# Attention's memory by last use, the second image's tokens in six tiles, the sum check among the experts, and three key pairs at first

## The chip, the cores and the metric

The kernel runs on one core of a Trainium2 chip. A core has five engines with a queue of instructions each: TensorE (PE, matrix products and transposes, with its own queue part PEld for loading the stationary operand), VectorE (DVE), ScalarE (ACT), GpSimd (POOL) and SyncE (SP, which here only issues DMA transfers). Engines wait for one another through semaphores. SBUF is the on-chip memory of 128 partitions, PSUM the banks that PE writes its products to, DRAM the memory outside. The metric is the device time of one execution in microseconds (us). The kernel before took 2222.04 us, the median of 4 runs between 2219.52 and 2223.07.

## What is computed

The input is two images of 256 channels and 56 x 56 pixels. Three blocks follow each other, each added to its input:

```python
x = x + conv_attention(group_norm(x))          # 1x1 conv to q,k,v; 3x3 depthwise conv; 7x7 neighbourhood
                                               # attention, 4 heads with dilation 1, 4 with 2; projection
t = to_tokens(x)                               # (2, 3136, 256)
t = t + linear_attention(layer_norm(t))
t = t + experts(layer_norm(t))                 # 8 experts, the best 2 of each token, H = 1024
x = from_tokens(t)

# linear_attention(x), per image, with h = 8 heads of 32:
Q = elu(x @ Wq) + 1;  K = elu(x @ Wk) + 1;  V = x @ Wv
KV = einsum('nshd,nshv->nhdv', K, V)           # one 32x32 matrix per head and image, over all tokens
Z = 1 / (einsum('nlhd,nhd->nlh', Q, K.sum(1)) + 1e-6)
msg = layer_norm(einsum('nlhd,nhdv,nlh->nlhv', Q, KV, Z) @ Wm)
msg = layer_norm(relu(concat(x, msg) @ W1) @ W2)
return x + msg
```

What matters below is that the linear attention of an image can take up its queries only when the keys of all that image's tokens are summed.

## The kernel before

The kernel has four stages. The *front* (`front()`, to about 810 us) does group norm, convolutions and neighbourhood attention in bands of rows, strip by strip. A finished strip is divided by its sums (`normalise`, whose reciprocals are stored to DRAM as `rb` at L567), projected on PE into a PSUM tile `s_ps` together with the input `x_s` (loaded at L758, transposed at L323), copied to `t_i` by DVE or ACT in turn (`evac`, L154) and stored as tokens to the DRAM array `td` (L772). There are 49 blocks of 128 tokens. The first 25 (`NA`) are the first image's, with half a block of the second. While the front finishes the second image, the first image's tokens are loaded again (`t_a`) and their keys are made (`first_keys`, L295).

The *keys* of two blocks, a pair, are made by `keys()` (L228), a generator in three parts: statistics on DVE, `rs` as a power on POOL (L225), the normalised `xt`, its transposes `pts` on PE and the copy to `xT_b`; then the product `kp` with `w_k` and `elu`+1 of it, `ks`; then the products `kx` of `ks` and `xt`, which PE sums up over the pairs in one PSUM tile, and the sum of `ks` in `acc` on POOL. `close_keys` and `merged` (L284, L1175) turn the sums into the two small matrices that queries use: transposes `kxt`, products with `w_v` (`kvt`, masked by DVE into `kvt_sb`), products with `w_m` (`mwp`), centred, and the diagonal blocks `ksm`. PE and DVE alternate there.

Between the front and the next stage stands `check_sums` (L821): it loads all stored reciprocals as `chk_r` (128 x 396), compares them with two bounds in four DVE operations, sums over the partitions with one product `chk_p` and writes a flag `bad`, read at the very end.

*Layer 1* (`layer1`, L1081, from 810 to about 1380 us) loads the second image's tokens into one tile `t_b` of 24 blocks by six transfers on SP (L199), its weights by transfers on POOL's queue (L1104), prepares the feed-forward's weights (`centre(fw2)`, the bias products `hb`, the scaling of `fw1`, L1140 to L1152), merges the first image's sums and then works on 14 groups of up to four blocks in a software pipeline of 18 steps (L1443). In step s, group s is in its queries (`q`: products `pq`, `elu`, then `pd` and the quotient), group s-1 in the message (`m`: products `pm` in L1262, then transposes `mts`), s-2 in the feed-forward (`f`), s-3 in routing (`r`), whose last part, the rows' scattering, comes in the step after (`p`). In each of the first six steps two key pairs of the second image (`u` and `v`) are made as well, and at the end of step 5 the second image's sums are closed and merged. PE's instructions stay in the order in which the program calls the parts (`manual_schedule`, L1441); this order is a string, one letter for each next part:

```python
for part in "mqfpufmuqfurfvrfvfv" if s < ng else "mfffpmfrfrff":
    next(on.get(part, iter(())), None)
```

A letter with no generator in this step does nothing. The first `pm` product of a step marks where it starts. The other engines' instructions are put in order by a scheduler of the framework.

The *experts* (loop at L1648, 53 tiles of 256 rows from about 1381 to 2146 us) gather rows (`xr`), transpose them (`px`), scale them (`xe`, DVE), multiply by `w1e` (`ph`, L1626) and `w2e` (`py`, L1634), add the bias (`yt`, DVE) and scatter the result. The last stage transposes the output back.

SBUF and PSUM are shared out in pools. A pool that closes frees its memory, and a later pool may lie on it. Where a later pool has nothing said of it, its first use waits for everything that ever used the memory beneath the whole pool; with `reuse_waits="tile"` a tile waits only for what used its own bytes. The front's pools (L342 to L350) and its two PSUM pools close together at its end; `rtb` and `p3w`, `p3k`, `p3s`, with the PSUM pools `p3pk`, `p3pa`, `p3pq`, `p3ph`, lie on their memory. The pools of the experts' weights have `reuse_waits="tile"` already.

## Time and profile before

| | us |
|---|---|
| median of 4 runs (2219.52 to 2223.07) | 2222.04 |
| the profiled execution | 2219.14 |
| its span, first to last instruction | 2217.4 |
| PE busy in the span (90%) | 2002.8 |
| DVE / ACT / POOL busy | 1016.2 / 620.2 / 688.7 |
| mean granted clock of PE | 0.952 |

By stage, from one answer on the engines' busy time in stretches (PE busy of the stretch's length, granted clock, share of the DMA engines):

| stretch, us | length | PE busy | clock | DMA |
|---|---|---|---|---|
| 0 to 776, front | 776.0 | 686.7 | 0.95 | 0.39 |
| 776 to 810, end of the front | 34.0 | 28.2 | 0.95 | 0.17 |
| 810 to 1381, layer 1 | 571.0 | 497.9 | 0.93 | 0.15 |
| 1381 to 2146, experts | 765.0 | 753.8 | 1.00 | 0.65 |
| 2146 to 2217.4, output | 71.4 | 36.3 | 0.61 | 0.61 |

How to read the profile: each line of a timeline gives the start of an instruction (or of several alike), its length, engine, line of the program, operation and operands by the program's names, and in brackets how long the engine had been idle before it and what released it. `SPq` and `POOL ... DMA_DIRECT2D` are issues of transfers; the time when the data land is another. A busy time of PE includes stretches at a lower granted clock, in which the same product takes up to twice as long; the clock column tells of these.

### The profile page before, as it was taken

Reading aid. Unit: us, or ns where it says so; the run is one execution under the profiler, and the core shown is the slowest. Engines: PE = TensorE matmul, PEld = TensorE weight load, DVE = VectorE, ACT = ScalarE, POOL = GpSimd, SP = SyncE. Lnnn points to the kernel's source line nnn. Section 1 sums busy time; section 2 is a strip of 40 time slices with the busy share of each in tenths; the row PEclk is TensorE's granted clock in tenths of the full one; section 3 lists DMA queues with packets and bytes.
Section 4 is the critical chain, followed back from the end, with each engine's and each line's share of the span. In section 5 each row is a group of like instructions: output and inputs, shape, how many; then the busy total and the mean of one; then the engine's idle time right before and its main releaser. Section 6 shows DMA issues by size and latency. Waiting matters only on the chain. (4 is left out here: it accounts for less than half of the span.)

```text
span 2217.4 us, 27966 instructions
## 1 busy us (share of the span) xinstructions
PE 2002.8 (90%) x10188; PEld 1403.7 (63%) x10188; DVE 1016.2 (46%) x2506; ACT 620.2 (28%) x1240; POOL 688.7 (31%) x806
## 2 busy tenths in 40 slices
PE   4899889999988867999999984999999999999994
PEld 2454444554444545666565673888888888888873
DVE  4877867875976544455455443211111111111111
ACT  1233323333323312433323321222222222222221
POOL 3821102111023423445344453223223333233320
PEclk9999989999989988999999996999999999999995
DMA  7642422343341140000011113866666666666627
GB/s 164 146 106 82 128 71 68 107 127 83 108 148 28 44 141 3 10 29 34 34 49 50 46 57 121 273 186 192 185 189 200 183 197 188 183 199 189 190 58 238
DMA packets 187682, 267.92 MB, mean 121 GB/s; under 512 B 24502, under 2 KB 146180, under 8 KB 187166
## 3 DMA queue, kind: packets, MB, share of 16 engines
q1 hardware_dynamic: 157374, 220.64, 32.1%
q0 software_dynamic: 21568, 31.26, 7.1%
q10 hardware_dynamic: 8592, 14.11, 2.4%
q8 instruction: 84, 1.38, 0.3%
q14 instruction: 64, 0.52, 0.1%
HBM read 199.02 MB, written 73.34 MB: 123 GB/s over the span
## 5 line engine op out<-in xcount | busy, mean ns | idle before, releaser
L1626 PE MATMUL ph<-xe,w1e 128*128 128x256 f32 x1696 | 379.7, 382 | 11.2 <-DVE xe L1618 11.2
L1634 PE MATMUL py<-w2e,hT 128*128 128x256 f32 x1696 | 374.7, 379 | 0.0
L1626 PEld LDWEIGHTS ph<-xe,w1e 128*128 128x128 f32 x1696 | 321.4, 191 | 60.8 <-DVE xe L1618 17.8
L1634 PEld LDWEIGHTS py<-w2e,hT 128*128 128x128 f32 x1696 | 322.2, 190 | 43.8
L1630 ACT ACTIVATE hT<-ph,sv 128x256 f32<-128x256 f32 x360 | 168.1, 473 | 488.1 <-PE ph L1626 485.7
L508 DVE SCALAR_TENSOR_TENSOR yc<-ypad,w,yc 128x1120 f32<-128x1120 f32 x192 | 267.8, 1398 | 50.9 <-ACT yc L506 47.9
L495 PE MATMUL pc<-ypad,diag 128*128 128x448 f32 x432 | 176.6, 549 | 0.5 <-ACT ypad L489 0.5
L1639 DVE TENSOR_TENSOR yt<-py,b2e 128x512 f32<-128x512 f32 x53 | 36.7, 692 | 303.8 <-PE py L1634 303.8
L145 POOL DMA_INDIRECT y<-yt,idi x106 | 167.2, 1577 | 26.1 <-issue 17.2
L483 PE MATMUL py<-x_sb,wq 128*128 128x448 f32 (+1 forms) x384 | 158.9, 545 | 17.5 <-ACT ypad L489 9.8
L539 DVE TENSOR_TENSOR p<-s_ps,tab 98x340 f32<-98x340 f32 (+5 forms) x240 | 138.1, 601 | 62.1 <-PE s_ps L535 60.3
L1641 POOL TENSOR_SCALAR yt<-yt,eq 128x256 f32<-128x256 f32 x106 | 49.4, 472 | 372.0 <-DVE yt L1639 372.0
L544 ACT ACTIVATE p<-p 98x680 f32<-98x680 f32 (+5 forms) x120 | 111.8, 932 | 170.2 <-DVE p L539 163.5
L535 PE MATMUL s_ps<-qT,kT 32*98 32x170 f32 (+5 forms) x960 | 129.8, 405 | 19.2 <-DVE p L539 17.3
L1600 DVE CAST idi<-xr 128x2 int32<-128x2 f32 x53 | 9.0, 169 | 289.9 <-DMA y<-yt,idi 289.9
L535 PEld LDWEIGHTS s_ps<-qT,kT 32*98 32x98 f32 (+1 forms) x960 | 57.2, 171 | 106.8 <-DVE p L539 60.8
L483 PEld LDWEIGHTS py<-x_sb,wq 128*128 128x128 f32 x384 | 71.5, 200 | 82.5 <-issue 55.5
L495 PEld LDWEIGHTS pc<-ypad,diag 128*128 128x128 f32 x432 | 78.2, 189 | 71.6 <-issue 68.2
L472 POOL TENSOR_SCALAR diag<-ident,w 128x128 f32<-128x128 f32 x108 | 84.0, 796 | 117.4 <-PE pc L495 110.4
L145 POOL DMA_INDIRECT xs<-row,si x98 | 96.3, 983 | 64.7 <-DVE si L1418 36.0
L225 POOL TENSOR_TENSOR rs<-rs,mhalf 128x2 f32<-128x2 f32 (+2 forms) x89 | 65.2, 739 | 117.4 <-DVE rs L224 107.2
L1292 PE MATMUL p<-m2T,fw 128*128 128x512 f32 (+2 forms) x224 | 95.2, 549 | 0.0
(281 smaller groups left out, 2635.8 us busy)
## 6 DMA issues: line engine op xcount, KB each, us to landing
w1e<-in_L_ffn_W SPq DMA_DIRECT2D x53, 1024.0 KB
w2e<-in_L_ffn_W SPq DMA_DIRECT2D x53, 1024.0 KB
yd<-yc SPq DMA_DIRECT2D x24, 784.0 KB
xr<-xs SPq DMA_DIRECT2D x53, 260.0 KB
ld<-yd SPq DMA_DIRECT2D x28, 448.0 KB
b2e<-in_L_ffn_b SPq DMA_DIRECT2D x53, 128.0 KB
yr<-y SPq DMA_DIRECT2D x12, 512.0 KB
out<-o_sb ACTq DMA_DIRECT2D x24, 256.0 KB
```

Source lines behind the costliest of these rows:

```text
L145: ins = nc.gpsimd.indirect_dma_start(out=dst[:, :], out_offset=bass.IndirectOffsetOnAxis(ap=index, axis=0), in_=src, in_offset=None, **kw,)
L472: nc.gpsimd.tensor_scalar(diag[:, tap, :], ident, w2[:, oc, tap : tap + 1], 1.0, ALU.mult, ALU.mult)
L483: nc.tensor.matmul(py[:, :n, :], wq1[:, ct, oc * P : (oc + 1) * P], x_sb[:, ct, (q0 + g0) * WW : (q0 + g0 + n) * WW], start=(ct == 0), sto ...
L495: nc.tensor.matmul(pc, diag[:, tap, :], ypad[:, dy : dy + 8, dx : dx + WW], start=(tap == 0), stop=(tap == 8),)
L508: nc.vector.scalar_tensor_tensor(yc[:, 8:, :], src, w, yc[:, 8:, :], ALU.mult, ALU.add)
L535: nc.tensor.matmul(s_ps[:nk, j, :n].rearrange("p (i j) -> p i j", j=nj), kT[hs], q[hs], start=True, stop=True,)
L539: nc.vector.tensor_tensor(p[:nk, 2 * pr : 2 * pr + 2, :n].rearrange("p h (i j) -> p h i j", j=nj), s_ps[:nk, :, :n].rearrange("p h (i j) - ...
L544: nc.scalar.activation(p[:nk, :, :n], p[:nk, :, :n], AF.Exp)
L1292: nc.tensor.matmul(p1[:, :w], fw1[:, k, oc * P : (oc + 1) * P], rhs, start=(k == 0), stop=(k == 3))
L1626: nc.tensor.matmul(p1, w1e[:, ct, j * P : (j + 1) * P], xe[:, ct, :], start=(ct == 0), stop=(ct == 1),)
L1630: nc.scalar.activation(hT[:, j, :], p1, AF.Gelu, bias=sv[:, 4 + j : 5 + j])
L1634: nc.tensor.matmul(py[:, h, :], hT[:, j, h * P : (h + 1) * P], w2e[:, j, :], start=(j == 0), stop=(j == NJ - 1),)
```

## The change

The diff does five things.

- The front's pools are declared in another order: `p2b` and `p2r` behind the pools of loaded rows, keys, values and tables. `rtb` and all pools of layer 1 get `reuse_waits="tile"`, and the four PSUM pools are declared in another order.
- `t_b` becomes a list of six tiles of four blocks; `at()` picks the tile.
- `check_sums` is called in the loop over expert tiles, ahead of tile 4, takes its tiles from the experts' pools (its product in the tag `pt`), and `bad` lies in the pool of constants.
- What prepared the feed-forward's weights becomes `prepare_feed_forward()`, called behind the parts of step 0.
- The second image's 12 key pairs come three in each of the steps 0 and 1, with the strings "quvuqvuvwww" and "mquvumvquwvww", and two in each of the steps 2, 3 and 4; the sums are closed and merged at the end of step 4 instead of 5.

```diff
--- before.py
+++ after.py
@@ -187,8 +187,10 @@
 
         def at(self, n0, n):
 
-            h = int(n0 >= NA)
-            return self.t[h][:, n0 - h * NA : n0 - h * NA + n, :]
+            if n0 < NA:
+                return self.t[0][:, n0 : n0 + n, :]
+            k = (n0 - NA) % 4
+            return self.t[1][(n0 - NA) // 4][:, k : k + n, :]
 
         def turned(self, n0, n):
 
@@ -339,14 +341,15 @@
 
 
         cv = ExitStack()
-        bp = ph.enter_context(tc.tile_pool(name="p2b", bufs=1))
+
         tbp = ph.enter_context(tc.tile_pool(name="p2t", bufs=1))
         ldp = ph.enter_context(tc.tile_pool(name="p2l", bufs=2))
         kp = ph.enter_context(tc.tile_pool(name="p2k", bufs=3))
         vp = ph.enter_context(tc.tile_pool(name="p2v", bufs=2))
         pp = ph.enter_context(tc.tile_pool(name="p2p", bufs=2))
+        rp_ = ph.enter_context(tc.tile_pool(name="p2r", bufs=1))
+        bp = ph.enter_context(tc.tile_pool(name="p2b", bufs=1))
         ac = ph.enter_context(tc.tile_pool(name="p2ac", bufs=2))
-        rp_ = ph.enter_context(tc.tile_pool(name="p2r", bufs=1))
         xp = ph.enter_context(tc.tile_pool(name="p2x", bufs=2))
         cw = cv.enter_context(tc.tile_pool(name="p1w", bufs=1, side="right"))
         yp = cv.enter_context(tc.tile_pool(name="p1y", bufs=2, side="right"))
@@ -818,28 +821,24 @@
         tokens.kw.close()
         return tokens
 
-    def check_sums():
-
-        cp = ctx.enter_context(tc.tile_pool(name="chk", bufs=1))
-        with ExitStack() as ph:
-            wp = ph.enter_context(tc.tile_pool(name="chk2", bufs=1))
-            ps = ph.enter_context(tc.tile_pool(name="chkp", bufs=1, space=PSUM))
-            n = NR // P
-            r = wp.tile([P, n], F32, name="chk_r")
-            nc.sync.dma_start(r, rb.rearrange("(p n) -> p n", p=P))
-            ok = wp.tile([P, n], F32, name="chk_ok")
-            nc.vector.tensor_scalar(ok, r, 1.0 / DEN_MAX, None, ALU.is_ge)
-            nc.vector.tensor_scalar(r, r, 1.0 / DEN_MIN, None, ALU.is_le)
-            nc.vector.tensor_tensor(ok, ok, r, ALU.mult)
-            okc = wp.tile([P, 1], F32, name="chk_c")
-            nc.vector.tensor_reduce(okc, ok, AX.X, ALU.add)
-            ones = wp.tile([P, 1], F32, name="chk_o")
-            nc.vector.memset(ones, 1.0)
-            pc = ps.tile([1, 1], F32, name="chk_p")
-            nc.tensor.matmul(pc, okc, ones, start=True, stop=True)
-            bad = cp.tile([1, 1], mybir.dt.int32, name="bad")
-            nc.vector.tensor_scalar(bad, pc, float(NR), None, ALU.is_lt)
-        return bad
+    bad = const.tile([1, 1], mybir.dt.int32, name="bad")
+
+    def check_sums(wp, ps):
+
+        n = NR // P
+        r = wp.tile([P, n], F32, name="chk_r")
+        nc.sync.dma_start(r, rb.rearrange("(p n) -> p n", p=P))
+        ok = wp.tile([P, n], F32, name="chk_ok")
+        nc.vector.tensor_scalar(ok, r, 1.0 / DEN_MAX, None, ALU.is_ge)
+        nc.vector.tensor_scalar(r, r, 1.0 / DEN_MIN, None, ALU.is_le)
+        nc.vector.tensor_tensor(ok, ok, r, ALU.mult)
+        okc = wp.tile([P, 1], F32, name="chk_c")
+        nc.vector.tensor_reduce(okc, ok, AX.X, ALU.add)
+        ones = wp.tile([P, 1], F32, name="chk_o")
+        nc.vector.memset(ones, 1.0)
+        pc = ps.tile([1, 1], F32, name="chk_p", tag="pt")
+        nc.tensor.matmul(pc, okc, ones, start=True, stop=True)
+        nc.vector.tensor_scalar(bad, pc, float(NR), None, ALU.is_lt)
 
     def attention_general(ph):
 
@@ -1081,8 +1080,8 @@
     def layer1(ctx, tk):
 
         run, cnt = tk.run, tk.cnt
-        rtp = ctx.enter_context(tc.tile_pool(name=f"rtb{run}", bufs=1))
-        tk.t[1] = rtp.tile([P, NF - NA, C], F32, name="t_b")
+        rtp = ctx.enter_context(tc.tile_pool(name=f"rtb{run}", bufs=1, reuse_waits="tile"))
+        tk.t[1] = [rtp.tile([P, 4, C], F32, name=f"t_b{i}") for i in range((NF - NA) // 4)]
 
         groups = [(4 * i, 4) for i in range(6)] + [(24, 1)] + [(25 + 4 * i, 4) for i in range(6)]
 
@@ -1091,13 +1090,12 @@
             tk.load(n0, n)
 
         with ExitStack() as ph:
-            wp = ph.enter_context(tc.tile_pool(name="p3w", bufs=1))
-            wk = ph.enter_context(tc.tile_pool(name="p3k", bufs=2))
-            sm = ph.enter_context(tc.tile_pool(name="p3s", bufs=3))
-            ps_k = ph.enter_context(tc.tile_pool(name="p3pk", bufs=1, space=PSUM))
-            ps_a = ph.enter_context(tc.tile_pool(name="p3pa", bufs=2, space=PSUM))
-            ps_q = ph.enter_context(tc.tile_pool(name="p3pq", bufs=2, space=PSUM))
-            ps_h = ph.enter_context(tc.tile_pool(name="p3ph", bufs=3, space=PSUM))
+            def pool(name, bufs, **kw):
+                return ph.enter_context(tc.tile_pool(name=name, bufs=bufs, reuse_waits="tile", **kw))
+
+            wp, wk, sm = pool("p3w", 1), pool("p3k", 2), pool("p3s", 3)
+            ps_h, ps_k = pool("p3ph", 3, space=PSUM), pool("p3pk", 1, space=PSUM)
+            ps_q, ps_a = pool("p3pq", 2, space=PSUM), pool("p3pa", 2, space=PSUM)
 
             def load(name, src, shape):
                 w = wp.tile(shape, F32, name=name)
@@ -1137,19 +1135,21 @@
                 nc.vector.tensor_scalar(m[:, :n], m[:, :n], 1.0 / C, None, ALU.mult)
                 nc.vector.tensor_tensor(w, w, m[:, :n].unsqueeze(2).to_broadcast([P, n, C]), ALU.subtract)
 
-            centre(fw2)
-
-            hb_ps = ps_h.tile([P, 512], F32, name="hb", tag="h")
-            for oc in range(4):
+            hb = wp.tile([P, 4], F32, name="hb_sb")
+
+            def prepare_feed_forward():
+                centre(fw2)
+
+                hb_ps = ps_h.tile([P, 512], F32, name="hb", tag="h")
+                for oc in range(4):
+                    for k in range(2):
+                        nc.tensor.matmul(
+                            hb_ps[:, oc : oc + 1], fw1[:, 2 + k, oc * P : (oc + 1) * P], g1b1[:, k, 1:2],
+                            start=(k == 0), stop=(k == 1),
+                        )
+                nc.vector.tensor_copy(hb, hb_ps[:, 0:4])
                 for k in range(2):
-                    nc.tensor.matmul(
-                        hb_ps[:, oc : oc + 1], fw1[:, 2 + k, oc * P : (oc + 1) * P], g1b1[:, k, 1:2],
-                        start=(k == 0), stop=(k == 1),
-                    )
-            hb = wp.tile([P, 4], F32, name="hb_sb")
-            nc.vector.tensor_copy(hb, hb_ps[:, 0:4])
-            for k in range(2):
-                nc.vector.tensor_scalar(fw1[:, 2 + k, :], fw1[:, 2 + k, :], g1b1[:, k, 0:1], None, ALU.mult)
+                    nc.vector.tensor_scalar(fw1[:, 2 + k, :], fw1[:, 2 + k, :], g1b1[:, k, 0:1], None, ALU.mult)
 
             tk.xT[1] = wp.tile([P, 2, (NF - NA) * P], F32, name="xT_b")
 
@@ -1436,6 +1436,8 @@
                 )
             ng = len(order)
             qzs, m2Ts = [], []
+            second = list(range(NA, NF, 2))
+            turns = "quvuqvuvwww", "mquvumvquwvww", "mqfpufmuqfurfvrfvfv"
 
 
             with tc.manual_schedule(engines={mybir.EngineType.PE}):
@@ -1450,12 +1452,14 @@
                         on["f"] = feed_forward(*order[s - 2], m2Ts.pop(0))
                     if 3 <= s < ng + 3:
                         on["r"] = route(*order[s - 3])
-                    if s < 6:
-                        for k in range(2):
-                            on["uv"[k]] = keys(tk, wk, sm, ps_a, 4, kx, acc, groups[7 + s][0] + 2 * k, 2)
-                    for part in "mqfpufmuqfurfvrfvfv" if s < ng else "mfffpmfrfrff":
+                    if s < 5:
+                        for part in "uvw" if s < 2 else "uv":
+                            on[part] = keys(tk, wk, sm, ps_a, 4, kx, acc, second.pop(0), 2)
+                    for part in turns[min(s, 2)] if s < ng else "mfffpmfrfrff":
                         next(on.get(part, iter(())), None)
-                    if s == 5:
+                    if s == 0:
+                        prepare_feed_forward()
+                    if s == 4:
                         kxs = wk.tile([P, 2, C], F32, name="kxs", tag="u")
                         kc = sm.tile([P, 2], F32, name="kc")
                         close_keys(tk, ps_a, kx, acc, kxs, kc)
@@ -1648,6 +1652,8 @@
             for t in range(NTL - NIF):
                 if t == 2:
                     make_tables()
+                if t == 4 and run == 0:
+                    check_sums(wp, ps_t)
                 expert_tile(t)
             behind = nc.values_load(
                 tables.last[0:1, 0:1], min_val=0, max_val=NDT,
@@ -1681,7 +1687,6 @@
 
     with ExitStack() as ph:
         tokens = front(ph)
-    bad = check_sums()
     with ExitStack() as ph:
         layer1(ph, tokens)
     bad = nc.values_load(
```

## The prediction

> **What bounds the kernel now.** The profiled execution took 2219.14 us (span 2217.4); the median shown is 2222.04, 2.90 us more. I sum against the first and add the 2.90 at the end. First the page, 40 slices of 55.4 us:
>
> ```profile
> PE   4899889999988867999999984999999999999994
> PEclk9999989999989988999999996999999999999995
> ```
>
> TensorE (PE) is the busy engine nearly everywhere. The holes are at the start, in slices 14 and 15 (776 to 887 us, where the front ends and layer 1 begins) and in slice 24, which the change doesn't touch. Next, the engines' busy time by stretch; the columns are start:end, length, then busy us (instructions) of PE, weight loads, DVE, ACT, POOL, the granted clock, the DMA share and GB/s:
>
> ```profile
> 774.00:793.05 19.05, 17.58 (x170) 11.32 (x170) 8.90 (x19) 6.29 (x11) 4.93 (x7) 1.00 0.00 1
> 810.00:855.50 45.50, 29.49 (x90) 19.24 (x91) 24.49 (x70) 6.08 (x10) 19.96 (x29) 0.73 0.46 140
> 855.50:884.00 28.50, 21.57 (x77) 14.93 (x76) 11.16 (x32) 9.11 (x22) 10.43 (x12) 0.90 0.00 0
> 884.00:922.80 38.80, 38.23 (x142) 25.12 (x142) 14.42 (x42) 13.85 (x34) 12.61 (x15) 1.00 0.02 7
> 965.00:1008.10 43.10, 41.51 (x170) 28.15 (x169) 24.77 (x92) 14.78 (x36) 24.42 (x29) 1.00 0.11 37
> 1008.10:1058.00 49.90, 46.16 (x194) 31.92 (x193) 27.41 (x98) 15.36 (x37) 25.82 (x30) 0.98 0.11 38
> 1058.00:1092.80 34.80, 34.13 (x130) 21.83 (x128) 16.88 (x65) 11.37 (x28) 12.65 (x16) 0.98 0.09 31
> ```
>
> Row 2 is step 0 (front's last matmul to the first `pm`): 16.0 us of PE idle, at 0.73 clock. Row 3 is step 1, 6.9 idle. From step 2 on PE is full: work there costs its full price, work in steps 0 and 1 may fall into holes. Note too that DMA is idle at 774 to 793 us. Who holds step 0, by PE's timeline (start, us, line, count; in brackets idle before and releaser):
>
> ```profile
> 810.55 0.63 PE L1185 MATMUL kxt<-ident,kxs 128*128 128x128 f32 x4 [0.61 <-DVE chk_o L837]
> 815.69 2.08 PE L1222 MATMUL pq<-xT_a,w_q 128*128 128x512 f32 x2 [4.51 <-DMA w_q<-in_L_attn_Wq]
> 829.84 1.22 PE L1196 MATMUL kvt<-kxt_sb,w_v 128*128 128x128 f32 x4 [6.26 <-DVE kvt_sb L1200]
> 830.86 3.41 PE L1145 MATMUL hb<-g1b,fw 128*128 128x1 f32 x16
> 838.26 3.78 PE L256 MATMUL kp<-w_k,xT_b 128*128 128x256 f32 x8 [0.68 <-ACT xT_b L158]
> 849.12 1.99 PE L256 MATMUL kp<-w_k,xT_b 128*128 128x256 f32 x8 [1.55 <-DVE xT_b L160]
> 853.18 2.54 PE L269 MATMUL kx<-xt,ks 128*128 128x256 f32 x8 [2.07 <-DVE ks L208]
> 855.52 4.79 PE L1262 MATMUL pm<-mw,qz 128*128 128x256 f32 x16
> ```
>
> The weights come late because POOL may not issue them before the front's whole memory is free; the second image's tokens (`t_b`) because SP's load waits for PE's check matmul at 818.12; `kvt_sb` because DVE first waits for tokens and then does 1.20 and 1.22 us on `fw`:
>
> ```profile
> 810.50 0.80 POOL L1104 DMA_DIRECT2D w_v<-in_L_attn_Wv  x1 [17.38 <-issue]
> ```
>
> ```profile
> 818.34 7.55 SPq L199 DMA_DIRECT2D t_b<-td  x6
> ```
>
> ```profile
> 825.73 0.75 DVE L216 BATCH_NORM_STATS2 st<-t_b 128x6 f32<-128x256 f32 x2 [3.10 <-DMA t_b<-td]
> 828.37 1.22 DVE L1138 TENSOR_TENSOR fw<-fw,wmean 128x1024 f32<-128x1024 f32 x1
> ```
>
> **Memory, waits and token tiles: the front's end.** In the changed order, SP's queue gets three `t_b` loads between the `rb` stores (762 to 797 us), three more between the last `x_s` loads and `td` stores. DVE gets the first pairs' statistics before its last normalising and `t_i` copies; POOL gets three `rs` powers before `w_v`. DVE's added work is about 6.5 us (ten statistics of 0.39 to 0.42, their aggregates at 0.16, small operations at 0.15, and waits of 0.72 for POOL's power); it lies largely in DVE's gaps (4.78 us before the 805.33 copy, 3.63 before 809.98). It holds the last `t_i` by 0.6 to 1.0. SP's fourth `t_b` load has to wait for the first `td` store to land (issued 801.0, landing 2.2 to 2.7 us later), and the last `x_s` load (803.9 in the trace, inside the pair at 802.76) and the later `td` stores queue behind it: `x_s` goes at some 807.9 and lands near 810.5. PE's last projections follow. I take the front's last matmul at 812.5 instead of 809.94; +1.6 if DVE's copies alone set it, +3.6 if the queue does. Moving `w_v` (about 804.5, was 810.50) and `w_q` (805.3) ahead of this lands them by 809; landing took 4.4 us at 810.5. So waits for weights end, while the front ends 2.5 later. The three early token tiles hold the six pairs of steps 0 and 1; the other three, landed by about 820, are due from step 2: no wait.
>
> **Step 0 rewalked.** PE's work after the last projection, at full clock: `kx` of the shared tile 0.6 (its row of 1.13 at half clock), `kvt` 1.5, eight `pq` 3.6 (step 1's row: 3.60 for eight), `mwp` 1.2, three pairs of `pts` 0.6, `kp` 1.99, `kx` 1.99 = 13.8, `pd` 1.9, `hb` 1.7 (3.41 at half clock): 24.2 us. `kxt` moves back into the hole before 796. Waits left: about 2.7 before the second `kvt` (`kvt_sb` now stands behind two `qz` of 0.69 and ACT's `elu`, without the 2.4 on `fw`), 0.7 before the first `kp`, 1.6 for the second pair, 2.1 for the third; 7.1 us. One stretch of 3.4 us at half clock costs 1.7. So 812.5+24.2+7.1+1.7 = 845.5, with small issue gaps 846.5, where `pm` was at 855.52. Bounds 842.5 (front +1.6, full clock, third pair's wait covered) to 851 (front +3.6, three half-clock stretches). Centring `fw2`, `hb` and the `fw1` scaling now follow step 0; their users are the feed-forward's products in step 2, some 25 us later, so DVE's 3.3 us are hidden by steps 0 and 1.
>
> **The clock, weighed.** Whether it drops is a matter of how full a 3.41 us window is:
>
> ```profile
> 847.66:851.07 3.41, 1.95 (x8) 1.00 0.02 5
> 851.07:854.48 3.41, 1.34 (x7) 1.00 0.00 0
> 854.48:857.90 3.42, 3.42 (x10) 0.50 0.00 0
> ```
>
> PE busy 1.34 us of a window was followed by a half-clock window; 1.95 was not. The longest single gap in the window at 851.07 is the 2.07 of the `kx` row.
> The Trainium skill, "TensorE: Matmul & The Clock Gate", section "HAM oscillation — how this bites in real kernels", states as its abstract rule "no PE-idle gaps >~3.4µs." By it none of the gaps I expect would throttle, and step 0 would end at 844.8; the trace differs, since gaps of 2.07 us cost a half-clock window here.
> I go by the row and charge one such window in step 0 and one in step 1.
>
> **Step 1** took 28.5 us with two pairs. Its half-clock share (0.90 granted) is 6.8 us of windows, 3.4 lost; full-clock work 18.2. A third pair adds 4.6, `hb`'s rest nothing: 22.8, plus the 6.9 idle less what the third pair fills, plus 1.7 for one half window: 29 to 32, taken 30.5. Step 2 then starts at 846.5+30.5 = 877.0 instead of 884.04: **7.0 gained** (bounds 0 and 14).
>
> **Steps 2 to 5.** Before, by the starts of `pm`: 38.7, 42.2, 43.1 and 49.9, the last with two pairs and the closing of the keys (`kxs`, `kxt`, `kvt`, `mwp`: 1050.2 to 1057.98 less its overlap, 6.9). Step 6, without keys, took 34.5. After: 38.7, 42.2, 43.1+6.9, 34.5 = 165.4 against 173.9: **8.5 gained**, which is two pairs of 4.3 us, (43.1-34.5)/2, moved out of full steps. Bounds 7 and 10. Step 6 reads the second sums one step later than they are made, as now.
>
> **Check among the experts.** Its border stay costs only 0.61 us directly. In its new place SP issues `chk_r` among the fills at about 1410; DVE's 0.37+0.52+0.57+0.57 = 2.03 us wait for it and stand before the second tile's `yt` (0.69 at 1414.28) and the third tile's `xe` (1414.89), which PE awaits. At a landing of 1412.7 to 1413.2, `xe` comes 0.9 later: **1 lost**, bounds 0 and 3 (if it lands 2 later). The later stages run the same instructions with the same waits: 0.
>
> Sum: 7.0+8.5-1.0 = 14.5 gained; 2204.6 by the profiled execution, 2207.5 by the median.
>
> **Rivals.**
> (1) *Denser than thought*: no half-clock window, the third pair filling the idle of steps 0 and 1. Step 0 then ends at 843 and step 1 takes 28.5: 12.5+8.5-1 = 20; 2202. For: three pairs offer PE work in each gap. Against: DVE and ACT must feed it.
> (2) *Collision at the border*: weights, tokens, `x_s` and `td` now share 800 to 815. DMA share was 1.08 at 820 to 830 with 321 GB/s, and the token loads took 5 us from issue there. Front's end +6 and step 0 then 850.5, step 1 32: 1.5+8.5-1 = 9; 2213.
> (3) *The weights still come late*: POOL's three powers ahead of `w_v` wait for DVE's statistics, which wait for the tokens. If `w_v` goes at 810 as before, the 4.5 us stay, and the front's end is later: about 1.5 of the 7.0 then stays: 1.5+8.5-1 = 9, less the tokens' own delay of 4 if `t_b` is late too: 5; 2217. Against: the first three token loads wait for stores long landed.
> (4) *Slower*: SP's fourth `t_b` load waits for a `td` store and holds the last `x_s`, so the last strips, so every later load. Each us of that wait beyond the 4 counted is a us lost. From 14.5 of it the change is worth nothing, from 19 it is slower; a store would have to land 19 us late, where 2.7 is the longest seen. I price it at 2228.
>
> **How the numbers follow.** Forecast 0.52, (1) 0.17, (2) 0.16, (3) 0.08, (4) 0.07. 0.2% is 4.4 us, about what a measurement of this kernel can tell. Faster: all of the first three but 0.02, and half of (3): 0.87; same: 0.06, that rest; slower 0.07. The range: all three terms at their worst and best give 4 to 24 us, together unlikely; I take 5 to 24 with (1), (2) and half of (3) inside, 2198 to 2217; (4) stays out.
>
> **What will show it.** `w_v` issued before 806 and no wait on `w_q`; last projection at 811.5 to 813.5; first `pm` of step 1 at 843 to 851; steps 2 to 5 together 165 us; step 5 34.5; one idle of about 1 us at the third expert tile. Wrong if the front's last matmul is past 816, if step 1 is over 33 us, or if closing the keys in step 4 exposes more than 7 us.

## The result, and the profile after

The changed kernel takes 2222.72 us (median of 52 runs), the kernel before 2217.91 (median of 78; the four runs shown ahead of the prediction lay 4 us above that). The ratio is 1.0023, with a 95% interval of 1.0016 to 1.003: 5 us slower, where a gain of 14.5 us was forecast and 2207.5 us, with 2198 to 2217 as the range. The time lies outside the range and the sign is wrong.

The profiled execution after took 2227.36 us, with a span of 2225.6 against 2217.4. Of these 8.2 us, 4.1 are there already at the last `kp` product of the first image's keys (start 793.8 us, before 789.7), up to which PE runs the same instructions in both. Two traces of one kernel differ by as much: in second traces of the two kernels, shown further down, the same product started at 798.8 (changed) and 795.1 (before). All positions below are therefore counted from this product, "the last first-image `kp`". From it to the start of step 6 the changed kernel takes 271.9 us and the kernel before 268.2; the rest of the program, from there to the end, differs by 0.5 (by 2.9 in the second traces).

The stages, from the engines' busy time by stretch of the changed kernel. The columns are start:end, length, busy us (instructions) of PE, weight loads, DVE, ACT and POOL, granted clock, DMA share and GB/s. The rows are PE's wait at the end of the front (its last projection included), the rest of step 0, step 1, step 2, step 4 (with the closing of the keys) and step 5:

```profile
812.40:823.10 10.70, 2.52 (x7) 1.40 (x6) 0.00 (x0) 1.07 (x2) 5.21 (x11) 0.74 0.99 330
823.10:862.90 39.80, 31.61 (x105) 22.38 (x105) 20.03 (x47) 7.30 (x12) 12.35 (x14) 0.76 0.10 20
862.90:898.90 36.00, 27.24 (x98) 19.66 (x99) 15.31 (x44) 10.54 (x24) 15.05 (x17) 0.87 0.00 1
898.90:937.60 38.70, 38.13 (x141) 25.07 (x140) 14.43 (x42) 13.85 (x34) 12.56 (x15) 1.00 0.02 7
979.90:1030.50 50.60, 46.86 (x193) 32.54 (x192) 27.49 (x98) 15.36 (x37) 25.78 (x30) 0.95 0.11 37
1030.50:1065.70 35.20, 34.52 (x130) 22.14 (x129) 16.89 (x65) 11.38 (x28) 12.65 (x16) 0.97 0.09 31
```

Row 1 is new: for 10.7 us PE has 2.5 us of work and the DMA engines are full (share 0.99, 330 GB/s). Row 2 is shorter than before (45.6), at a clock that is hardly better (0.76, before 0.73). Row 3 is 36.0 where before it was 28.5. The last rows hold the gain: step 5 without keys takes 35.2, step 4 takes over the closing.

PE's timeline of the changed kernel shows the waits behind rows 1 to 3 (start, us, line, products; in brackets idle before and releaser):

```profile
820.74 0.65 PE L325 MATMUL s_ps<-ident,x_s 128*112 128x128 f32 x2 [8.17 <-DMA x_s<-in_x]
823.70 2.04 PE L1433 MATMUL kx<-shared 64*128 64x256 f32 x4 [0.61 <-DVE t_i L160]
826.69 5.82 PE L1222 MATMUL pq<-xT_a,w_q 128*128 128x512 f32 x8
835.17 1.22 PE L1196 MATMUL kvt<-kxt_sb,w_v 128*128 128x128 f32 x4 [2.66 <-DVE kvt_sb L1200]
877.90 2.81 PE L258 MATMUL kp<-w_k,xT_b 128*128 128x256 f32 x8 [3.41 <-DVE xT_b L160]
890.12 0.44 PE L240 MATMUL pts<-ident,xt 128*128 128x128 f32 x2 [2.50 <-DVE xt L139]
897.06 1.99 PE L271 MATMUL kx<-xt,ks 128*128 128x256 f32 x8 [2.13 <-DVE ks L210]
```

The waits for weights are gone, as forecast (`pq` follows at once). In their place stands a wait of 8.17 us for the front's own last input, and `kx` and `pq` behind it run at half clock (2.04 and 5.82 us where full clock takes 1.1 and 3.6). In step 1 PE waits 3.41, 2.50 and 2.13 us for DVE's part of the three pairs' chains.

What the last `x_s` load met, by SP's timeline (issues) and POOL's:

```profile
808.77 0.38 SPq L201 DMA_DIRECT2D t_b<-td  x1
809.93 1.00 SPq L775 DMA_DIRECT2D td<-t_i  x2
811.03 0.77 SPq L761 DMA_DIRECT2D x_s<-in_x  x1
```

```profile
808.01 0.80 POOL L1102 DMA_DIRECT2D w_v<-in_L_attn_Wv  x1
810.26 1.50 POOL L1102 DMA_DIRECT2D fw<-in_L_attn_W  x2
```

It is issued behind the fourth token load (512 KB) and at the same time as 2.3 MB of weights, and PE gets it 9.7 us after its issue. Among the experts the check does what was forecast, 0.92 us: PE's wait for the third tile's `xe` was 0.36 and is 1.28, in the changed kernel's PE timeline:

```profile
1423.98 6.31 PE L1630 MATMUL ph<-xe,w1e 128*128 128x256 f32 x28 [1.28 <-DVE xe L1622]
```

### The profile page after: what moved, and what is told of

It reads as the page before. It is cut to its first block, busy times and chain, and to the rows that moved or that the text cites. A ratio compares the mean times of both kernels' runs of the same rounds, so it can differ in the third digit from the quotient of the medians.

```text
span 2225.6 us, 27965 instructions
## 1 busy us (share of the span) xinstructions
PE 2007.3 (90%) x10188; PEld 1407.8 (63%) x10188; DVE 1016.0 (46%) x2506; ACT 620.2 (28%) x1240; POOL 690.9 (31%) x806
## 4 chain that ended last, share of the span: by engine, by line
PE 33%; issue 25%; DVE 14%; POOL 14%; DMA 5%; ACT 3%; SPq 0%; POOLq 0%; DVEq 0%; ACTq 0%
POOL y L145 7%; PE p L1292 4%; PE po L551 4%; PE pc L498 4%; PE py L486 3%; DVE yc L511 3%; PE s_ps L538 3%; POOL yt L1645 2%; POOL rs L227 2%; DVE p L542 2%; PE kp L258 2%; PE s_ps L330 2%; PE kx L271 2%; DMA yr<-y 1%; PE ph L1630 1%
## 5 line engine op out<-in xcount | busy, mean ns | idle before, releaser
L145 POOL DMA_INDIRECT y<-yt,idi x106 | 167.0, 1575 | 26.1 <-issue 17.2
L538 PE MATMUL s_ps<-qT,kT 32*98 32x170 f32 (+5 forms) x960 | 127.9, 403 | 20.3 <-DVE p L542 18.5
```

Source lines behind the costliest of these rows:

```text
L145: ins = nc.gpsimd.indirect_dma_start(out=dst[:, :], out_offset=bass.IndirectOffsetOnAxis(ap=index, axis=0), in_=src, in_offset=None, **kw,)
L538: nc.tensor.matmul(s_ps[:nk, j, :n].rearrange("p (i j) -> p i j", j=nj), kT[hs], q[hs], start=True, stop=True,)
```

## The experiments

All stretches are in us, from one trace each. "Front" is the end of the front's last matmul behind the last first-image `kp`; "step 0" is the rest of step 0, from there to the first `pm`; the last column is from that `kp` to the start of step 6, which sums the four.

| kernel | ratio to before (95%) | front | step 0 | step 1 | steps 2-5 | to step 6 |
|---|---|---|---|---|---|---|
| before | 1 | 20.2 | 45.6 | 28.5 | 173.9 | 268.2 |
| before, second trace | | 19.7 | 44.9 | 27.0 | 174.3 | 265.9 |
| changed | 1.0023 (1.0016 to 1.003) | 29.3 | 39.8 | 36.0 | 166.8 | 271.9 |
| changed, second trace | | 31.6 | 37.5 | 36.0 | 166.8 | 272.0 |
| e1: fw late | 0.9992 (0.997 to 1.0015) | 26.7 | 33.0 | 35.2 | 166.8 | 261.7 |
| e2: tokens behind x_s | 1.002 (1.0001 to 1.0039) | 20.2 | 42.8 | 35.2 | 166.9 | 265.1 |
| e3: both | 0.9978 (0.9957 to 0.9998) | 19.8 | 36.2 | 35.3 | 167.1 | 258.3 |
| e4: old turns | 1.0033 (1.0013 to 1.0053) | 30.2 | 35.3 | 29.4 | 173.0 | 267.9 |
| e5: tokens and fw late | 0.9991 (0.9973 to 1.001) | 20.3 | 35.5 | 35.3 | 166.9 | 258.1 |
| e6: e5 with old turns | 0.9965 (0.995 to 0.998) | 24.7 | 31.2 | 29.3 | 173.5 | 258.6 |
| e14: e6 again | 0.9984 (0.9966 to 1.0001) | 24.5 | 28.6 | 29.2 | 173.5 | 255.6 |
| e7: e5, all weights late | 0.9993 (0.9976 to 1.001) | 19.7 | 38.8 | 35.8 | 165.5 | 259.7 |
| e8: before with new turns | 1.0041 (1.0022 to 1.006) | 20.2 | 50.0 | 35.0 | 166.8 | 271.9 |
| e9: e6, statistics behind t_i | 0.9987 (0.9972 to 1.0002) | 20.1 | 36.2 | 27.5 | 174.0 | 257.8 |
| e10: e9 with new turns | 0.9997 (0.9983 to 1.0011) | 20.7 | 38.6 | 35.4 | 166.9 | 261.6 |
| e11: e4, statistics behind t_i | 0.9993 (0.9975 to 1.0011) | 21.4 | 37.2 | 29.4 | 173.1 | 261.1 |
| e12: e9, mask loaded early | 0.9968 (0.9956 to 0.9981) | 20.5 | 28.6 | 29.1 | 173.6 | 251.8 |
| e12, second trace (e17) | | 19.9 | 32.4 | 29.2 | 173.9 | 255.3 |
| e13: e12 with new turns | 0.9985 (0.997 to 1.0) | 20.5 | 34.7 | 35.7 | 167.1 | 258.1 |

### What held the front's end: e1, e2 and e3

Theory C says that the early transfers share the DMA engines with the front's last load; rival Q says that the load's place in SP's queue makes it late. e1 moves 1.5 MB of weights, e2 moves token loads, e3 does both. In the diffs `tk.behind(...)` gives what it encloses a place in its engine's order behind a named instruction: "x_s" is the last `x_s` load, "tokens" the last `td` store, "copy" DVE's last copy to `t_i`.

e1:

```diff
-            fw1 = load("fw1", rows("L1_attn_W1"), [P, 4, 2 * C])
-            fw2 = load("fw2", rows("L1_attn_W2"), [P, 4, C])
+            fw1 = wp.tile([P, 4, 2 * C], F32, name="fw1")
+            fw2 = wp.tile([P, 4, C], F32, name="fw2")
+            with tk.behind("tokens"):
+                nc.sync.dma_start(fw1, rows("L1_attn_W1"))
+                nc.sync.dma_start(fw2, rows("L1_attn_W2"))
```

> The changed kernel, but the two large feed-forward weights (fw1 and fw2, 1.5 MB of the 2.3 MB of weights) are issued from SP's queue behind the last store of tokens instead of from POOL's queue ahead of the last input load. Theory C (collision): the last x_s load, which took 9 us from issue (811.0) to its user on PE (820.7), was late because the weights' transfers shared the DMA engines with it; then it lands within 4.5 us of its issue, PE's gap before the last projection falls from 8.2 us to under 4, and the kernel takes 4 to 8 us less than the changed one (2222.7): 2215 to 2219, ratio to before 0.999 to 1.000. Rival Q (queue): the load was late because of what stands ahead of it on SP (the fourth token load and two token stores); nothing of that moves, so the landing stays 8 to 10 us behind and the time within 2 us of the changed kernel: 2221 to 2225.

e2:

```diff
-        for n0, n in groups[7:]:
+        for n0, n in groups[7:10]:
             tk.load(n0, n)
+        with tk.behind("x_s"):
+            for n0, n in groups[10:]:
+                tk.load(n0, n)
```

> The changed kernel, but the last three token loads are queued on SP behind the last x_s load, which also goes ahead of two token stores, as before the change. Theory C and rival Q both expect the x_s load to be issued some 4 us earlier relative to the projections, ahead of the weights, and PE's gap of 8.2 us to fall under 2; the front's last matmul then comes 8 us earlier and the kernel takes 2213 to 2217 (ratio 0.998 to 1.000). If neither holds (the load waits for PE to free its buffer, and is issued as late as now), the gap stays over 6 us and the time stays 2221 to 2225.

e3 (both diffs):

> Both edits of the first two runs together. Theory C with the clock as the second step (the 8 us gap put PE at half clock for the 30 us behind it, which made the rest of step 0 39.8 us where 34 was forecast): the gap goes, and with it the half clock; the rest of step 0 (front's last matmul to the first pm) falls to 34 to 36 us, step 1 to 31 to 34, and the kernel takes 2207 to 2213 (ratio 0.995 to 0.998). Rival D (the third pair is what PE waits for: DVE and ACT cannot feed it): the rest of step 0 stays 38 to 40 and step 1 35 to 37, and only the gap is won: 2213 to 2217.

In e1 PE's wait for the load fell from 8.17 to 5.72 us, not under 4, and the kernel took 0.9992 of the time before: C by sign and size of the time, but only some third of the wait went with these 1.5 MB. That share is rough: with the loads where the change has them the wait was 9.60 us in the changed kernel's second trace and 4.86 in e4. In e2 the load was issued ahead of the fourth token load, the wait fell to 0.28, and the front's last matmul was back at 20.2 us. Yet the time did not move (1.002), which neither had expected: the wait had moved on by one transfer. In e2's PE timeline

```profile
826.20 2.04 PE L1441 MATMUL kx<-shared 64*128 64x256 f32 x4 [6.89 <-DVE t_i L160]
```

and in its DVE timeline

```profile
825.62 0.42 DVE L160 COPY t_i<-s_ps 112x256 f32<-112x256 f32 x1 [9.70 <-DMA td<-t_i]
```

PE waits for DVE's last copy to `t_i`, and that waits until a store of tokens has landed and freed the tile, under the same traffic. e3 wins both waits in part (`kx` waits 5.02 us). So the place in SP's queue and the traffic both count, and a repair of one alone only hands the wait to the next transfer of the front.

### The traffic alone: e5 and e7

e5 puts the last three token loads, too, behind the last `td` store; e7 puts `w_v`, `w_q` and `w_m` there as well.

```diff
-        with tk.behind("x_s"):
+        with tk.behind("tokens"):
             for n0, n in groups[10:]:
                 tk.load(n0, n)
```

```diff
-            w_v = load("w_v", rows("L1_attn_Wv"), [P, 2, C])
...
-            fw2 = load("fw2", rows("L1_attn_W2"), [P, 4, C])
+            with tk.behind("tokens"):
+                w_v = load("w_v", rows("L1_attn_Wv"), [P, 2, C], nc.sync)
...
+                fw2 = load("fw2", rows("L1_attn_W2"), [P, 4, C], nc.sync)
```

> The changed kernel with the last three token loads and the two feed-forward weights all queued on SP behind the last store of tokens; of the large transfers only w_v, w_q and w_m (768 KB) are left beside the front's last loads and stores. Theory C (the transfers share the DMA engines, so each megabyte that goes meanwhile delays the last loads and stores): the store of tokens that the last copy to t_i waits for, which took 7.5 us in the run with both edits (816.0 to 823.5), takes under 5; PE's idle before the shared kx falls from 5.0 to under 3 us, and from the last first-image kp to step 6 it takes 252 to 256 us (258.3 there, 271.9 in the changed kernel); time 2211 to 2216, ratio 0.995 to 0.998. Rival W (the small weights alone do it): the store still takes over 6.5 us, nothing is gained on the run with both edits: 2215 to 2219.

> As the kernel with late token loads, and w_v, w_q and w_m queued on SP behind the last tokens and the token loads too: nothing large goes beside the front's last loads and stores. What they cost alone is then seen: by theory C the last x_s load lands within 3 us of its issue, the last stores within 4, and the front's last matmul comes 18.5 to 20.5 us behind the last first-image kp (20.2 before the change, 29.3 after it). The weights are then what step 0 waits for, some 8 to 10 us, so the time is no better than before: 2216 to 2224. By rival W's opposite (the slowness is the queue's or the buffers', not the traffic's) the landings stay at 7 us or more.

With e5 the wait for `t_i` fell from 5.02 to 1.75 us (under 3, as C had it); to step 6 it took 258.1 us, no less than e3, because 2.92 us of waiting for `kvt_sb` came back; the time is not to be told from before (0.9991). In e7 nothing large goes beside the front's last transfers, and the front ends 19.7 us behind the `kp`, as C had it; PE then waits for the weights, by e7's PE timeline, as before the change:

```profile
820.11 1.19 PE L1205 MATMUL kvt<-kxt_sb,w_v 128*128 128x128 f32 x4 [7.94 <-DMA w_v<-in_L_attn_Wv]
```

Of this wait of 8 us little is left at step 6, though: e7 gets there only 1.6 us later than e5 (259.7 and 258.1), and their times are alike. Early weights together with early tokens cost the front 9 to 12 us. By the traces' semaphore updates the last `x_s` load landed 2.8 us after its issue in the kernel before, 9.6 in the changed one (11.5 in its second trace), 6.9 in e1, 4.6 in e2, 4.0 in e3, 3.3 in e5 and 2.5 in e7: the less goes beside it or the earlier it goes, the sooner it lands. The Trainium skill, "DMA: Bandwidth & Descriptors", section "Issuing engines are not separate DMA queues", has it that queues of different engines run on the same 16 DMA engines and interleave. The runs agree: with 2.3 MB issued by POOL and 512 KB of tokens beside it, the load issued by SP reached PE 9.7 us after its issue; in e7, with all of these behind it, PE took it up 4.1 us after its issue (804.0 to 808.13) and did not wait for it.

### The turns: e4, e6, e8, e10 and e13

The turns were undone in the changed kernel (e4), in e5 (e6), and put alone into the kernel before (e8); e10 and e13 are e9 and e12 with the new turns. The edit in e4 and e6 is

```diff
-            turns = "quvuqvuvwww", "mquvumvquwvww", "mqfpufmuqfurfvrfvfv"
+            turns = ("mqfpufmuqfurfvrfvfv",) * 3
...
-                    if s < 5:
-                        for part in "uvw" if s < 2 else "uv":
+                    if s < 6:
+                        for part in "uv":
...
-                    if s == 4:
+                    if s == 5:
                         kxs = wk.tile([P, 2, C], F32, name="kxs", tag="u")
```

and in e8 it is the reverse, on the kernel before.

> The changed kernel with the old turns: two key pairs in each of six steps, sums closed in step 5; everything else as changed. If the third pairs fill holes (the prediction), the steps 2 to 5 take 7 to 8.5 us more and the steps 0 and 1 give back 2 to 3: 2227 to 2229. Rival D (a third pair costs as much in steps 0 and 1 as in the full steps): steps 0 and 1 give back 6.6 and 6 to 7.5, and the time is 2216 to 2219, less than the changed kernel.

> As the last kernel, with the old turns (two pairs in six steps). The traces of the changed kernel and of the one with the old turns, put at full clock, say that a third pair costs 4.0 us in step 0 and 6.8 in step 1 and that two pairs less save 6.3 in the steps 2 to 5: so the old turns are worth 4 us here, 2207 to 2213, and from the last first-image kp to step 6 it takes 3 to 5 us less than with the new turns. Rival H (holes, as predicted): the new turns are the better ones by 3 to 6 us also here, 2216 to 2221.

> The kernel before with the new turns alone (three pairs in the steps 0 and 1, sums closed in step 4); memory, waits, tiles, check and the preparation as before. By the prediction's own prices a third pair costs 6.7 us in step 0 and 2 in step 1 against 8.5 saved later: no difference, 2216 to 2220. By the prices at full clock in the traces (4.0 and 6.8 against 6.3): 4 to 5 us slower, 2221 to 2224, ratio 1.002 to 1.003. If the 16 us of PE idle in step 0 can take up the pair: 4 to 6 us faster, 2212 to 2215.

e8 is the plain answer: the turns alone make the kernel before 0.41% slower (0.22 to 0.60), 9 us. The rows of the table give the account. A third pair makes step 1 longer by 6.0 to 8.0 us in every comparison (35.0 to 36.0 with three pairs, 27.0 to 29.4 with two) and the rest of step 0 by 2.2 to 6.9; it saves 6.2 to 7.5 in the steps 2 to 5. To step 6 that is 3.7 to 6.0 us lost in e8. In e4 the trace says the same (267.9 against 271.9 and 272.0 with the new turns), but the times don't show it: 1.0033 and 1.0023, whose intervals overlap. e5 against e6 and e14 is 0.9991 against 0.9965 and 0.9984. The ratio with the new turns is thus the higher one in four of five comparisons (e10 and e13 below).

### What was left: e9, e11, e12, e10, e13

In e6 the front still ended 24.7 us behind the `kp`, since POOL issued `w_v`, `w_q` and `w_m` behind two `rs` powers that wait for DVE's statistics, and so beside the last `x_s` loads (`w_v` 12.6 us behind the `kp`, the last `x_s` 14.2), for which PE waited 4.49 us. e9 queues the statistics of step 0's pairs behind DVE's last copy to `t_i`, which puts the weights ahead of the powers; e11 does the same without the late loads.

```diff
                     for part in turns[min(s, 2)] if s < ng else "mfffpmfrfrff":
-                        next(on.get(part, iter(())), None)
+                        with tk.behind("copy") if s < 1 and part in "uvw" else ExitStack():
+                            next(on.get(part, iter(())), None)
```

> As the kernel with late token and feed-forward loads and the old turns, with one edit more: the statistics of step 0's key pairs are queued on DVE behind the last copy to t_i. DVE's last copies then come as before the change, and on POOL w_v, w_q and w_m are issued ahead of the rs powers that wait for these statistics, some 7 us earlier. If DVE's added statistics and POOL's order were the rest of the front's delay (point 1 of the prediction put 0.6 to 1.0 us to them), the front's last matmul comes 19 to 20.5 us behind the last first-image kp (24.7 there), no wait on weights is left, step 6 starts 252 to 255 us behind that kp (258.6 there), and the kernel takes 4 us less: ratio to before 0.994 to 0.9955. If they were not: 258 to 260, ratio 0.996 to 0.997. A loss is possible too: the statistics now wait in front of step 0's first transposes, 1.5 us for a pair.

> The changed kernel with the old turns and the statistics behind the last copies, but the token and feed-forward loads where the change has them. Theory C (the large transfers beside the last loads and stores are the first cause): the front's last matmul stays 25 to 30 us behind the last first-image kp and the time within 3 us of the kernel with the old turns alone (ratio 1.001 to 1.003). Rival P (DVE's statistics and POOL's order were it): 20 to 21, ratio 0.995 to 0.997.

The front's end was repaired in e9 (20.1) and nearly in e11 (21.4), where `fw1` and `fw2` now came later too, behind the powers; so the front's end went as P had it, but e11 does not separate the two theories, since what C blames had moved as well. But neither got faster than e6: step 0 took 36 to 37 us. e9's PE and DVE timelines show why:

```profile
829.66 1.23 PE L1207 MATMUL kvt<-kxt_sb,w_v 128*128 128x128 f32 x4 [6.39 <-DVE kvt_sb L1211]
```

```profile
828.92 0.48 DVE L1192 TENSOR_SCALAR ksm<-m,kc 128x128 f32<-128x128 f32 x2 [4.18 <-DMA m<-in_c_m]
```

The mask `m32`, 64 KB, stood on POOL behind the powers that had now become late; DVE needs it for `ksm` and `kvt_sb`. It was issued at 822.60 us and DVE had it at 828.92, 6.3 us later, beside the late feed-forward loads. e12 loads it from ACT's queue, which issues it at 812.16:

```diff
-            m32 = load("m32", a["c_m32"], [P, P])
+            m32 = wp.tile([P, P], F32, name="m32")
+            nc.scalar.dma_start(m32, a["c_m32"])
```

> As the kernel with the statistics behind the last copies (old turns, token and feed-forward loads late), with the mask m32 (64 KB) loaded from ACT's queue instead of POOL's, where it stood behind two rs powers and landed so late that PE waited 6.4 us for kvt_sb. If that wait is what ate the gain of the repaired front's end, it falls to under 2 us, PE keeps its clock, the rest of step 0 takes 26 to 30 us (36.2 there), step 6 starts 247 to 252 us behind the last first-image kp (257.8 there), and the ratio to before is 0.992 to 0.9955. If another wait takes its place, the rest of step 0 stays over 32 us and the ratio at 0.997 to 1.000.

> The last kernel with the new turns. Theory D (a third pair costs more in steps 0 and 1 than it saves in full steps): 4 to 5 us slower than the last kernel, step 0 and step 1 together 10 to 12 us longer, steps 2 to 5 6.3 shorter. Rival H (with the front's end in order and the clock up, the third pair fills holes): 2 to 6 us faster than it.

> The last kernel with the new turns: what the turns alone cost where no transfer is late. Theory D (a third pair costs 4 and 6 to 8 us in steps 0 and 1 and saves 6.3 in all later): 3 to 6 us slower than the last kernel. Rival H (the third pairs fill the holes of steps 0 and 1): 2 to 6 us faster than it.

In e12 the wait fell from 6.39 to 1.80 us, PE kept its clock, and the rest of step 0 took 28.6, by e12's PE timeline:

```profile
818.16 0.71 PE L1208 MATMUL kvt<-kxt_sb,w_v 128*128 128x128 f32 x4 [1.80 <-DVE kvt_sb L1212]
```

In its second trace (e17) it took 32.4, with 8.2 us of it at half clock where the first had 3.4. The stretches of e12's first trace (rest of step 0 and step 1), by the engines' busy time:

```profile
813.10:841.80 28.70, 20.49 (x86) 14.07 (x85) 19.94 (x62) 5.36 (x10) 14.69 (x21) 0.94 0.44 133
841.80:870.90 29.10, 22.14 (x79) 15.06 (x79) 12.03 (x35) 9.11 (x22) 10.42 (x12) 0.88 0.00 0
```

and of e13, the same with the new turns:

```profile
820.60:855.30 34.70, 24.35 (x105) 17.11 (x104) 25.13 (x74) 7.16 (x13) 20.25 (x26) 0.95 0.37 110
855.30:891.00 35.70, 26.09 (x98) 18.56 (x98) 15.56 (x44) 10.34 (x24) 15.08 (x17) 0.90 0.00 1
```

The clock is nearly the same in these two, so what the third pairs cost is seen bare: 6.0 us in step 0, of which 3.9 are PE's work and 2.1 idle, and 6.6 in step 1, 3.9 and 2.7 (against e12's second trace 2.3 and 6.5). e12 takes 0.9968 of the time before (0.9956 to 0.9981), less than was expected to be won (0.992 to 0.9955); with the new turns it is 0.9985. e6 was as fast in its first measurement (0.9965), but on e12's chip (e14) its median was 2214.04 us where e12 took 2209.49. e10 against e9 (0.9997, 0.9987) says the same by 0.1%, inside its intervals.

### Second traces: e14 to e17

e14 is e6 once more; e15, e16 and e17 are the kernel before, the changed one and e12, unchanged, for a second trace.

> The kernel with late token and feed-forward loads and the old turns once more, beside the two others on one chip, since its interval (0.995 to 0.998) and that of the kernel with the statistics moved (0.9972 to 1.0002) came from different calls: 0.9955 to 0.9975 again if the first measurement holds. If the statistics' place makes no difference in itself it stands 2 to 8 us above the kernel with the mask loaded early.

> The kernel before, unchanged, profiled once more, to see how far one trace of a kernel stands for it. The time that an edit at the border can move is the stretch from the last first-image kp to the start of step 6 (268.2 us in the first trace); expected again 266 to 270, while the time up to that kp (789.7 in the first trace, 789 to 800 in the runs with the changed layout) may differ by some 10 us through the clock. If it is near 790 again and near 797 with the changed layout, the layout slows the front itself, which no theory had.

> The changed kernel, unchanged, profiled once more: from the last first-image kp to step 6 again 270 to 274 us (271.9), the last x_s load again 8 to 10 us from its issue to PE; the time up to that kp anywhere from 788 to 800 if that part is chance, 793 or more if the layout slows it.

> The kernel with the mask loaded early, profiled once more: from the last first-image kp to step 6 again 250 to 254 us (251.8).

The last first-image `kp` started at 795.1 us in the second trace of the kernel before, at 798.8 in that of the changed one and at 788.3 in that of e12 (first traces 789.7, 793.8, 792.7): up to that point traces of one kernel differ by 4 to 5 us. Whether the new layout slows the front stays open: the sixteen traces with it have this product at 788.3 to 800.1 us, 795.0 in the mean, the three with the old layout at 789.6 (e8), 789.7 and 795.1. The stretch to step 6 repeats to 0.1 us in the changed kernel, 2.3 in the one before and 3.5 in e12, whose 255.3 is outside the 250 to 254 expected. So the border's account (3.7 to 6.1 us lost) meets the measured 5 us. For e12 it says 10.6 to 16.4 us won, and the times say 4.2 to 9.8: between the middles some 6 us are not accounted for. The experts' stretch, from the first tile's transposes to the output, was 788.8 and 788.0 in the kernel before and 790.1 and 790.5 in e12, 1.3 to 2.5 us more, the check's 0.9 among them; the rest stays open. It isn't e12's alone: all the kernels of the table but the changed one and e6 gain some 4 to 8 us less by their times than by the stretch to step 6 (or lose as much more), against the mean of the two traces of the kernel before; e8, with the old layout, too. So the stretches tell what happens at the border, and the times alone what a version is worth.

## Why the prediction was wrong, point by point

Two terms of the sum failed above all: the landing of the last `x_s` load with the moved transfers beside it (put at 2.6 us; PE had it after 9.7) and the third pair's price in step 1 (put at 2.0 us; 6.0 to 8.0 measured).

- **The landing of the last `x_s` load was mis-sized.** The part on the front's end issued it at "some 807.9" and let it land "near 810.5". The issue was right (17.2 us behind the `kp`, forecast 18.2), the 2.6 us of landing were not: PE got it 9.7 us after its issue, and in the second trace of the changed kernel the front ended later still. The 2.6 us are about what the same load took in the kernel before, with no weights beside it (issued at 803.9, last semaphore update at 806.7, first used at 808.70; the product at 806.51 waits for the load before it). In the same paragraph the first of 2.3 MB of weights were moved beside it. The front ended 9.1 us later instead of 2.5 (in the second pair of traces 11.9). Rival (2) named the collision, with 6 us and a chance of 0.16, and came nearest at the front; but it too had the change win 9 us.
- **Other landings were read too short.** The prediction gives a `td` store 2.2 to 2.7 us and calls 2.7 the longest seen. But DVE's copy waited 4.3 us from the issue of its store (801.03), by the DVE timeline of the kernel before:

```profile
805.33 1.02 DVE L160 COPY t_i<-s_ps 112x512 f32<-112x512 f32 x2 [4.78 <-DMA td<-t_i]
```

Rival (2) gives a token load 5 us; the one issued at 818.34 released DVE at 825.73, 7.4 us later.

- **The clock followed.** One half-clock window was charged to step 0. Of the rest of step 0 19.3 us ran at half clock, with PE busy in 18.1 of them: 9.0 us lost where 1.7 were charged. The gap of 8 us made a window with no product in it, and half clock lasted from 817.49 to 831.14 us, 8.0 of it in the rest of step 0; 6.8 more follow a window with 1.35 us of PE work, in which the wait for `kvt_sb` lies, and 4.4 come at the step's end. The walk itself was nearly right: put at full clock PE's work was 22.6 us where 24.2 were forecast, and its idle time 8.2 where 8.1 were, the small issue gaps included (the 1.13 us of `kx`, read as half clock, were at full clock). With no transfer late and the same turns (e13) the rest of step 0 takes 34.7, and 34.0 was forecast.
- **Step 1 was mis-sized.** The 30.5 us were 22.8 of work, 1.7 for the clock and the 6.0 that are left, idle. Measured were 22.6 of work, 4.6 lost to the clock and 8.8 idle, 36.0 together, and 35.0 to 35.8 in the other kernels with three pairs, whatever the transfers did. So the work was priced right, and the idle and the clock were not. The third pair found no holes, because the holes are the pairs' own waits, for DVE in the rows above: it brought its own (2.7 us more idle in e13's step 1 than in e12's).
- **Steps 2 to 5** were right but for 1.4 us: 166.8, forecast 165.4.
- **The turns were never summed by themselves.** By the prediction's own prices a third pair cost 6.7 us in step 0 and 2.0 in step 1, against 8.5 saved: nothing. The gain stood in the sum through the earlier start of step 0 alone, and no rival had the turns lose. By e12 and e13 they cost 12.6 and save 6.5 (8.8 and 6.8 by e12's second trace).
- **The weights** were issued 14.2 us behind the `kp`, as forecast (804.5 is 14.8), and PE no longer waited for them; rival (3) fell. **Rival (4)**, the queue on SP, was half of the truth: e2 shows that the load goes ahead if it is queued ahead, but not that this saves time.
- **The check**: 0.92 us, forecast 1.0.
- **The preparation behind step 0** was costed, for DVE, at nothing, as hidden behind step 0. DVE did its two long operations on `fw2` within step 0 (840.71 and 845.96 us, 1.21 us each). No run isolates what that costs.

Put together: 14.5 us forecast as won, less 6.6 (front), 5.8 (rest of step 0), 5.5 (step 1) and 1.4 (steps 2 to 5), is a loss of 4.8 us; the traces show 4.2 behind the `kp` and the times 5.

## What to carry to other kernels

When a transfer is moved into a stretch where the DMA engines look idle, list every small load and store of that stretch that some engine waits for, and price each with the new traffic beside it: here early weights took away a wait of 4.5 us in the kernel before (7.9 in e7), and together with the early tokens they made the front end 9 to 12 us later, through one input load and two stores. A hole on the busy engine takes up moved work only if that work doesn't wait on the same helpers as the work around the hole; price the moved part at its old and its new place side by side. And after each repair look for the next wait in line before the repair is judged: here it went from the input to the store, to the weights and to a 64 KB mask, and of the four kernels run side by side at the end (before, e12, e13, e14) the one that served all of them was the fastest.

## What the runs showed of the hardware

A half-clock window comes from how little PE did in the 3.41 us before it, not from one long gap. In e12, where no transfer is late, three such pairs lie in steps 0 and 1, by the engines' busy time of PE alone (length, PE busy, granted clock, DMA share, GB/s):

```profile
826.65:830.06 3.41, 1.21 (x5) 1.00 0.01 2
830.06:833.48 3.42, 3.32 (x11) 0.50 0.00 0
850.54:853.95 3.41, 1.49 (x10) 1.00 0.00 0
853.95:857.36 3.41, 3.41 (x9) 0.50 0.00 0
864.19:867.60 3.41, 1.33 (x7) 1.00 0.01 2
867.60:871.02 3.42, 3.42 (x9) 0.50 0.00 0
```

The longest single gaps in the first window of each pair are 2.2, 1.5 and 2.1 us. The border is fairly sharp: in the stretch from 780 to 1420 us of all nineteen traces, cut into the 3.41 us windows at whose edges the clock changes, half clock followed all 135 full-clock windows with less than 1.4 us of PE work, 29 of the 59 with 1.4 to 1.72, and 4 of the 2938 with more. The abstract rule of the Trainium skill that was weighed in the prediction (gaps of more than about 3.4 us) would have kept all three at full clock; the measurement decides, and the row of the trace before was the better guide.

What had not been expected is how far small transfers stretch: from the issue of a `td` store to the copy to `t_i` that it holds up it took 4.3 us in the kernel before (801.03 to 805.33) and 8.9 in e2 (815.22 to ACT's copy at 824.13), where the DMA engines were busy for a share of 0.96 (815.0 to 825.6 us, 321 GB/s).
